# A rational convolution layer: third and fifth power in one VectorE instruction, and the sets of powers in steps inside the loop

## The chip, the core and the metric

The kernel runs on one core of a Trainium2 chip. The core has five engines that run side by side, each through its own instructions in order: TensorE (PE, matmuls, with PEld for its weight loads), VectorE (DVE), ScalarE (ACT), GpSimd (POOL) and SyncE (SP), which here only issues DMAs. They work on the on-chip memory SBUF (128 partitions)[...]. Larger buffers lie in DRAM and are reached by DMA.

The metric is the device time of one launch in microseconds (us). A profiled execution gives a trace: each instruction with its start, its duration and what ended the wait before it.

## What is computed

Four layers, each a residual step on an image batch of 8 x 16 x 128 x 128 in float32. The change is in the third, `L2` of the reference:

```python
x = x + _L2_conv_ref(_gn(x), L2_conv_A, L2_conv_Bc)

def _L2_conv_ref(x, A, Bc):          # K = 3, DEG_P = 6, DEG_Q = 4
    ...
    wins = jnp.stack([xp[:, :, i:i + H, j:j + W] for i in range(K) for j in range(K)])
    pw = wins[..., None] ** jnp.arange(DEG_P, dtype=x.dtype)
    P = jnp.einsum('pbchwi,fcpi->fpbchw', pw, A)
    Q = 1.0 + jnp.abs(jnp.einsum('pbchwi,fcpi->fpbchw', pw[..., 1:1 + DEG_Q], Bc))
    out = jnp.sum(P / Q, axis=(1, 3))
```

`_gn` normalizes the image in groups. For every pixel, window position, input channel and output channel there is a ratio of two polynomials of the normalized value; the ratios are summed over window positions and channels. The powers 1 to 5 of the normalized image are what the polynomials are made from.

## The kernel before

**Powers.** `x` stays in SBUF as 128 partitions (8 images by 16 channels) of 128 x 128 pixels. `powers(r0)` (line 929) makes a set: the powers 1 to 5 of two rows. Two small memsets on GpSimd blank the left and right edge; VectorE normalizes (L934); ScalarE squares for the second and the fourth power (L942, L944); GpSimd multiplies for the third and fifth (L943, L945). Five DMAs on SyncE's queue (L947) write the set into the DRAM tensor `yd2`, which has, for each group of four channels, the five powers of these as 20 rows. Each power has one SBUF tile, so two sets don't overlap. 64 sets make the image.

**Loads.** `turn(r0, g)` (line 955) reads ten rows of `yd2` back into four tiles `f`, with 16 DMAs on SyncE (L959), so that powers and channels lie on partitions. There are eight `f` tiles, two groups `g` of four; while one group is used, the other is loaded. Ten DMAs (L927) write a zero row above and below the image at the layer's start.

**The loop.** A turn is eight rows; it has two groups `g` (which images), two row blocks `k` of four rows, nine window positions `n`, two pairs of images `i`. Each combination is a `Couple`: 16 x 2 x 2 x 9 x 2 = 1152 of them. A couple is worked as follows, with quarter and half tiles of 128 x 2048 values:

- TensorE: `denominators` (L971, pd), `numerators` (L971, pn), and `over_channels` (L1062), which sums finished ratios into the accumulators.
- ScalarE: `absolute` twice (L1009, t from pd), `ln` and `exp` (L152, u), which make 1/Q as exp(-ln Q).
- VectorE: `step` (L1020, a product of t and u for a correction of that reciprocal), `times` twice (L1030), `ratio` (L1034).
- GpSimd: `correction` (L1043, v from t and u), made to wait for the next couple's step (`apart`, "shared port").

Tiles t and u have four buffers, v three; pd and pn one each. At the end of a row block VectorE adds the accumulator to `x` and takes statistics (L1074, L1075).

**What sets the order.** The program is not run in the order in which it is written: a scheduler orders each engine's instructions by their dependences. An order by hand is put on it with `in_turn(engine, ins)`, which ties an instruction to the one given before it under the same name. In the loop all of VectorE's four, ScalarE's four and TensorE's instructions of a couple are tied so ("dve", "act", "pe2"). The instructions of `powers` and `turn` are not tied to anything, and the trace has them where the scheduler put them. In the text five sets are made before the first load, three more before the loop, and then four at the first couple of each turn (line 1103), with `turn` at the first couple of each group.

Of the kernel before, what the change touches and what calls it, by code (L numbers as in the profile page):

```python
# [9 lines left out]
F32 = mybir.dt.float32  # L10
AF = mybir.ActivationFunctionType
# [5 lines left out]
B, C, H, W = 8, 16, 128, 128  # L17
BC = B * C
HW = H * W
HP, WP = H + 2, W + 2  # L20
# [80 lines left out]
def kernel(  # L101
# [20 lines left out]
    nc = tc.nc  # L122
# [6 lines left out]
    dram = ctx.enter_context(tc.tile_pool(name="scratch", bufs=1, space=DRAM))  # L129
# [11 lines left out]
    sets = {AF.Exp: "exp_ln", AF.Ln: "exp_ln", AF.Tanh: "sigmoid", AF.Sigmoid: "sigmoid"}  # L141
# [68 lines left out]
    def in_turn(engine, ins):  # L210

        if engine in chain:
            tc.add_manual_dep(ins, chain[engine].name, order, reason="in turn")
        chain[engine] = ins
        return ins
# [3 lines left out]
    for n in range(5):  # L219
        t = cpool.tile([BC, BC], F32, name=f"w1_{n}")  # L220
        nc.gpsimd.memset(t, 0.0)
        for b in range(B):
            r = slice(b * C, (b + 1) * C)
# [10 lines left out]
    with ExitStack() as l0:  # L234
        wp = l0.enter_context(tc.tile_pool(name="w0", bufs=1))
        with tc.tile_pool(name="x0", bufs=2) as xp:
# [6 lines left out]
            mean0, _, rs0, d0 = group_stats(bn0, "0")  # L243
# [25 lines left out]
        for a in range(2):  # L269
            src = aff_d[:, a : a + 1].rearrange("(d p g c) a -> p g c (d a)", p=2, g=2, c=C)  # L270
            for odd in range(2):
                for g in range(2):
                    for i in range(3):
                        r = 64 * (g ^ odd) + 16 * i
# [6 lines left out]
        for i in range(3):  # L281
            for g in range(2):
                r = slice(64 * g + i * 16, 64 * g + i * 16 + 16)
# [44 lines left out]
        act = l0.enter_context(tc.tile_pool(name="act0", bufs=1))  # L328
        tmp = l0.enter_context(tc.tile_pool(name="tmp0", bufs=1))
# [326 lines left out]
        for n in range(-2, NCH + 3):  # L656
# [62 lines left out]
            if any((new, old, ahead)):  # L719
                r = var.finish()  # L720
# [43 lines left out]
    with ExitStack() as l1:  # L764
# [50 lines left out]
        for s in range(4):  # L815
            for p in range(2):
                if 0 <= s - p < 3:
# [4 lines left out]
                    for g in range(2):  # L822
# [3 lines left out]
                            k_("image")[rows, 2 * s + g : 2 * s + g + 1],  # L826
                        )

        mean, dm, rs, _ = group_stats(bn1, "1")
        xmax = wp.tile([BC, 1], F32, name="xmax")  # L830
        nc.vector.tensor_reduce(xmax, top, AX.X, ALU.max)
# [82 lines left out]
    with ExitStack() as l2:  # L914
# [2 lines left out]
        gather = k_("gather").rearrange("p (k g m) -> p k g m", k=2, g=2)  # L917
        mean, _, rs, _ = group_stats(bn2, "2")


        yd2 = dram.tile([4 * B, 20, HP, WP], F32, name="yd2")
        yv = yd2.rearrange("g (i c) h w -> g i c h w", i=5)
        zt = wp.tile([BC, WP], F32, name="zt")
        nc.gpsimd.memset(zt, 0.0)
        for i in range(5):
            for r in (0, HP - 1):
                nc.sync.dma_start(yv[:, i, :, r, :], zt)  # L927

        def powers(r0):

            y = [tmp.tile([BC, 2, WP], F32, name=f"y{i}") for i in range(1, 6)]
            nc.gpsimd.memset(y[0][:, :, 0:1], 0.0)
            nc.gpsimd.memset(y[0][:, :, WP - 1 : WP], 0.0)
            nc.vector.tensor_scalar(  # L934
                y[0][:, :, 1 : 1 + W],
                x[:, r0 * W : (r0 + 2) * W].rearrange("p (a b) -> p a b", a=2),
                mean,
                rs,
                ALU.subtract,
                ALU.mult,  # L940
            )
            nc.scalar.activation(y[1], y[0], AF.Square)  # L942
            nc.gpsimd.tensor_mul(y[2], y[1], y[0])  # L943
            nc.scalar.activation(y[3], y[1], AF.Square)  # L944
            nc.gpsimd.tensor_mul(y[4], y[3], y[0])  # L945
            for i in range(5):
                nc.sync.dma_start(yv[:, i, :, 1 + r0 : 3 + r0, :], y[i])  # L947

# [1 line left out]
        for t in fs:  # L952
            nc.gpsimd.memset(t, 1.0)

        def turn(r0, g):
            for q in range(NP):
                for u in range(4):
                    lo = 32 * (u ^ (q % 2))
                    nc.sync.dma_start(  # L959
                        fs[g * NP + q][lo : lo + 20],  # L960
                        yd2[4 * (2 * q + g) + u, :, r0 : r0 + 10, :],
                    )
# [120 lines left out]
            for i in range(NP // 2)  # L1083
        ]
        count = len(couples)
        for r in range(0, 10, 2):
            powers(r)
        turn(0, 0)
        for r in range(10, 16, 2):
            powers(r)  # L1090
        for c in couples[:2]:
            for ab in range(2):
                c.denominators(ab)
# [4 lines left out]
        for m in range(count + 2):  # L1098
            before, c, then, far, next_ = (
                couples[i] if 0 <= i < count else None for i in range(m - 1, m + 4)  # L1100
            )
            if c:
                if (c.k, c.n, c.i) == (0, 0, 0):
                    if c.g == 0 and c.r0 + 16 < H:
                        for r in range(c.r0 + 16, c.r0 + 24, 2):
                            powers(r)
                    if c.r0 + 8 * c.g < H:
                        turn(c.r0 + 8 * c.g, 1 - c.g)
                c.exp()
                c.step()  # L1110
                c.numerators()
            if far:
                far.absolute(0)
                far.denominators(1)
            if then:
                then.ln()
            if m % 2:
                if m >= 3:
                    over_channels(couples[m - 3 : m - 1], 2)
            elif 2 <= m <= count:  # L1120
                over_channels(couples[m - 2 : m], 1)
                over_channels(couples[m - 2 : m], 0)
            if far:
                far.absolute(1)
            if next_:
                next_.denominators(0)
            if before:
                before.correction(c.stepped if c else before.stepped)
            if c:
                c.times()  # L1130
                c.ratio()
# [353 lines left out]
```

## Time and profile before

| | |
|---|---|
| Time, median of 3 runs | 10728.44 us (10727.74 to 10730.07) |
| The profiled execution | 10728.63 us |
| Its span in the trace | 10726.8 us |
| TensorE busy | 9016.0 us (84%) |
| VectorE busy | 8720.1 us (81%) |
| ScalarE busy | 8613.6 us (80%) |
| GpSimd busy | 5545.4 us (52%) |
| Granted TensorE clock, mean | 0.976 |

The page divides the span into 40 slices of 268 us and gives each engine's busy share in tenths (9 is 90% or more):

```profile
PE   4999999999998568888888888888888888888799
...
DVE  3555555555555569999999999999999999999977
ACT  2555555555554679999999999999999999999988
POOL 3655655555553555555555555555555555555522
```

Slices 0 to 12 are the first layer and the second; the rational layer begins in slice 13 and ends near slice 37; the rest is the fourth layer. The fourth section of the page names the chain that ended last, followed back from the last instruction:

```profile
DVE 42%; PE 24%; issue 21%; ACT 7%; POOL 3%; DMA 2%; SPq 1%; ACTq 0%; DVEq 0%; POOLq 0%
PE banks L360 18%; DVE u L1030 15%; DVE pn L1030 10%; DVE u L1034 8%; DVE y L518 2%; DVE t L1020 2%; PE pn L971 2%; PE pd L971 2%; PE acc L1334 1%; POOL y L527 1%; DVE x L538 1%; ACT u L152 1%; DMA yd<-y 1%; ACT hid L152 1%; SPq L1298 1%
```

Rows of the couple's instructions (line, engine, operation, output from inputs, shapes, count; busy time and mean of one in ns; idle time before them and what ended it):

```profile
L1043 POOL TENSOR_TENSOR v<-t,u 128x1280 f32<-128x1280 f32 x1152 | 3374.3, 2929 | 2990.1 <-DVE t L1020 2960.8
...
L1020 DVE SCALAR_TENSOR_TENSOR t<-t,u 128x2048 f32<-128x2048 f32 x1152 | 2637.5, 2289 | 34.8 <-ACT u L152 25.2
L1009 ACT ACTIVATE t<-pd 128x1024 f32<-128x1024 f32 x2304 | 2348.6, 1019 | 86.6 <-POOL v L1043 42.3
L152 ACT ACTIVATE u<-u 128x2048 f32<-128x2048 f32 x1152 | 2200.4, 1910 | 0.0
L152 ACT ACTIVATE u<-t 128x2048 f32<-128x2048 f32 x1152 | 2192.1, 1903 | 0.0
...
L1030 DVE TENSOR_TENSOR u<-pn,u 128x1280 f32<-128x1280 f32 x1152 | 1718.1, 1491 | 39.4
```

Busy times count an instruction from its start to its end; two in a row on one engine can overlap by some hundredths of a microsecond. The names in "out<-in" are those of the tiles; several layers have a tile y.

### The profile page before, as it was taken

The page shows a single profiled execution, that of the slowest core. Times are in us where ns is not written, and L with a number is a line of the kernel's source. Part 1 is how long each engine was busy: PE and PEld are TensorE (multiplying, and loading weights), DVE is VectorE, ACT ScalarE, POOL GpSimd, SP SyncE. Part 2 cuts the span into 40 slices and gives each one's busy share as a digit, 9 for nine tenths or more (in the row PEclk, how much of TensorE's full clock was granted, in tenths as well). Part 3 has the DMA queues.
Part 4 walks back from the last instruction along what each step waited for, and adds up shares of the span by engine and source line. Part 5 has one row for each costly group of instructions (what it writes and reads, how often), then busy time and mean ns, then how long its engine had stood idle before and what let it go on. Part 6 is the DMA issues. An engine that isn't in the chain of part 4 may idle for free.

```text
span 10726.8 us, 191623 instructions
## 1 busy us (share of the span) xinstructions
PE 9016.0 (84%) x81588; PEld 2440.6 (23%) x81588; DVE 8720.1 (81%) x6829; ACT 8613.6 (80%) x7107; POOL 5545.4 (52%) x2681
## 2 busy tenths in 40 slices
PE   4999999999998568888888888888888888888799
PEld 1222222222222112222222222222222222222222
DVE  3555555555555569999999999999999999999977
ACT  2555555555554679999999999999999999999988
POOL 3655655555553555555555555555555555555522
PEclk8999999999999789999999999999999999999999
DMA  1000000000001320000000000000000000000022
GB/s 50 14 14 12 16 13 14 15 13 13 16 10 44 96 87 8 14 7 8 14 8 7 14 8 8 14 7 8 14 8 8 14 8 7 14 8 8 7 62 61
DMA packets 189456, 205.04 MB, mean 19 GB/s; under 512 B 46776, under 2 KB 155448, under 8 KB 186552
## 3 DMA queue, kind: packets, MB, share of 16 engines
q1 hardware_dynamic: 179944, 190.68, 6.7%
q8 instruction: 641, 10.50, 0.4%
q10 hardware_dynamic: 8656, 2.11, 0.1%
q14 instruction: 215, 1.76, 0.1%
HBM read 107.15 MB, written 60.04 MB: 16 GB/s over the span
## 4 chain that ended last, share of the span: by engine, by line
DVE 42%; PE 24%; issue 21%; ACT 7%; POOL 3%; DMA 2%; SPq 1%; ACTq 0%; DVEq 0%; POOLq 0%
PE banks L360 18%; DVE u L1030 15%; DVE pn L1030 10%; DVE u L1034 8%; DVE y L518 2%; DVE t L1020 2%; PE pn L971 2%; PE pd L971 2%; PE acc L1334 1%; POOL y L527 1%; DVE x L538 1%; ACT u L152 1%; DMA yd<-y 1%; ACT hid L152 1%; SPq L1298 1%
## 5 line engine op out<-in xcount | busy, mean ns | idle before, releaser
L1043 POOL TENSOR_TENSOR v<-t,u 128x1280 f32<-128x1280 f32 x1152 | 3374.3, 2929 | 2990.1 <-DVE t L1020 2960.8
L971 PE MATMUL pd<-f,wb 32*64 32x512 f32 x18432 | 2518.4, 610 | 332.8 <-ACT t L1009 301.0
L1020 DVE SCALAR_TENSOR_TENSOR t<-t,u 128x2048 f32<-128x2048 f32 x1152 | 2637.5, 2289 | 34.8 <-ACT u L152 25.2
L1009 ACT ACTIVATE t<-pd 128x1024 f32<-128x1024 f32 x2304 | 2348.6, 1019 | 86.6 <-POOL v L1043 42.3
L152 ACT ACTIVATE u<-u 128x2048 f32<-128x2048 f32 x1152 | 2200.4, 1910 | 0.0
L152 ACT ACTIVATE u<-t 128x2048 f32<-128x2048 f32 x1152 | 2192.1, 1903 | 0.0
L971 PE MATMUL pn<-f,wa 32*64 32x512 f32 x18432 | 1324.8, 624 | 938.4 <-DVE u L1034 938.1
L1030 DVE TENSOR_TENSOR u<-pn,u 128x1280 f32<-128x1280 f32 x1152 | 1718.1, 1491 | 39.4
L152 ACT ACTIVATE hid<-banks 128x1024 f32<-128x1024 f32 x576 | 571.4, 1023 | 1046.6 <-PE banks L360 1044.7
L527 POOL TENSOR_TENSOR y<-y 128x1536 f32<-128x1536 f32 x256 | 894.7, 3495 | 830.9 <-DVE y L518 830.9
L1062 PE MATMUL acc<-u,const 128*32 128x512 f32 (+2 forms) x13824 | 1118.9, 456 | 0.0
L1030 DVE TENSOR_TENSOR pn<-pn,u 128x768 f32<-128x768 f32 x1152 | 1104.2, 959 | 0.0
L1034 DVE SCALAR_TENSOR_TENSOR u<-t,pn 128x768 f32<-128x768 f32 x1152 | 1087.6, 944 | 0.0
L518 DVE TENSOR_TENSOR y<-banks,vp 128x1536 f32<-128x1536 f32 x384 | 672.9, 1752 | 274.0 <-PE banks L360 271.8
L971 PEld LDWEIGHTS pd<-f,wb 32*64 32x64 f32 x18432 | 512.1, 131 | 1610.2 <-ACT t L1009 1548.7
L1062 PE MATMUL acc<-v,const 128*32 128x512 f32 (+1 forms) x9216 | 749.9, 443 | 1.5 <-POOL v L1043 1.5
L544 ACT ACTIVATE sq<-x 128x1024 f32<-128x1024 f32 x384 | 397.9, 1054 | 412.3 <-DVE x L538 289.7
L971 PEld LDWEIGHTS pn<-f,wa 32*64 32x64 f32 x18432 | 279.5, 131 | 1947.3 <-DVE u L1034 1936.7
L470 POOL TENSOR_TENSOR pd<-q,kp 128x1536 f32<-128x1536 f32 (+1 forms) x256 | 693.6, 2733 | 8.0 <-PE banks L360 7.2
L360 PE MATMUL banks<-att,const 32*128 32x512 f32 x2304 | 497.3, 667 | 173.5 <-DVE att L509 95.9
L360 PE MATMUL banks<-h,wfc 64*128 64x512 f32 (+1 forms) x3072 | 618.4, 631 | 14.5 <-DVE h L606 14.5
L606 DVE TENSOR_TENSOR h<-banks,x 128x1024 f32<-128x1024 f32 x192 | 232.6, 1211 | 435.5 <-ACT hid L152 230.4
(182 smaller groups left out, 8068.9 us busy)
## 6 DMA issues: line engine op xcount, KB each, us to landing
f<-yd SPq DMA_DIRECT2D x512, 101.6 KB
yd<-y SPq DMA_DIRECT2D x320, 130.0 KB
xin<-in_x SPq DMA_DIRECT2D x752, 32.0 KB
four<-sil SPq DMA_DIRECT2D x256, 65.0 KB
xj<-in_x SPq DMA_DIRECT2D x8, 1024.0 KB
xl<-in_x SPq DMA_DIRECT2D x32, 256.0 KB
x1d<-xl SPq DMA_DIRECT2D x32, 256.0 KB
x<-x1d SPq DMA_DIRECT2D x8, 1024.0 KB
```

Source lines behind the costliest of these rows:

```text
L152: ins = nc.scalar.activation(out_, in_, func, **kw).ins
L360: in_turn("pe", mm(*args, skip_group_check=True, **kw).ins)
L470: ins = nc.gpsimd.tensor_mul(t[:, :n].rearrange("p n (a b) -> p n a b", a=4), rows(self.q[d][:, k]).unsqueeze(1).to_broadcast([128, n, 4, W]),
L518: ins = nc.vector.tensor_mul(y.rearrange("p n (a b) -> p n a b", a=4), banks[:, 1:4].rearrange("p n (a b) -> p n a b", a=4), windows(v, j, 3),
L527: in_turn("pool", nc.gpsimd.tensor_add(self.y[k], self.y[k], y).ins)
L971: yield mm(p[64 * (u % 2) : 64 * (u % 2) + 64, u // 2], w[lo : lo + 32, q % 2, n].rearrange("p c f -> p (c f)"), fs[g * NP + q][lo : lo + ...
L1009: in_turn("act", nc.scalar.activation(self.t[:, ab], self.pd, AF.Abs).ins)
L1020: ins = nc.vector.scalar_tensor_tensor(self.t, self.t, 1.0, self.u, op0=ALU.add, op1=ALU.mult).ins
L1030: in_turn("dve", nc.vector.tensor_mul(u if cols.start else p, p, u).ins)
L1034: ins = nc.vector.scalar_tensor_tensor(u, t, 2.0, p, op0=ALU.subtract, op1=ALU.mult).ins
L1043: ins = nc.gpsimd.tensor_mul(self.v, t, u).ins
L1062: ins = mm(accs[k][32 * q : 32 * q + 32, lo % 512 : (hi - 1) % 512 + 1], gather[:, int(part == 1), g], flat(c.u)[:, ab, lo:hi] if src is N ...
```

## The change

- The five powers of a set lie in one tile instead of five. The third and fifth power are made by one VectorE instruction: powers 2 and 4 times power 1, repeated. GpSimd keeps the two edge memsets.
- `powers` becomes a generator of four steps: normalize; square; square; product and the five DMAs. Its VectorE and ScalarE instructions are tied with `in_turn` to the loop's.
- In the loop a set is begun in every half of a turn's group, that is for each `g` and `k`, with one step at each of the first four window positions, at the first pair of images, ahead of that couple's exponential and step.
- `turn` is called at the fifth window position of a group instead of the first.
- The first eight sets use buffers of the loop's tiles t and u, and go side by side, three, then two, then three. Two of their five DMAs each go to ScalarE's queue, and every second one of the first turn's loads.
- The zero rows are written before the second layer's statistics, and from a tile with five rows of zeros.

```diff
+        yd2 = dram.tile([4 * B, 20, HP, WP], F32, name="yd2")
+        yv = yd2.rearrange("g (i c) h w -> g c i h w", i=5)
+        zt = wp.tile([BC, 5, WP], F32, name="zt")
+        nc.gpsimd.memset(zt, 0.0)
+        for r in (0, HP - 1):
+            for i in range(5):
+                nc.sync.dma_start(yv[:, :, i, r, :], zt[:, i])
+
         mean, dm, rs, _ = group_stats(bn1, "1")
...
-        for i in range(5):
-            for r in (0, HP - 1):
-                nc.sync.dma_start(yv[:, i, :, r, :], zt)
...
-            y = [tmp.tile([BC, 2, WP], F32, name=f"y{i}") for i in range(1, 6)]
-            nc.gpsimd.memset(y[0][:, :, 0:1], 0.0)
-            nc.gpsimd.memset(y[0][:, :, WP - 1 : WP], 0.0)
-            nc.vector.tensor_scalar(
-                y[0][:, :, 1 : 1 + W],
+        def powers(r0, name):
+
+            if name:
+                y = tmp.tile([128, 2, 2, 512], F32, name=name, bufs=4)
+                y = y.rearrange("p a b c -> p (a b c)")[:, : 10 * WP]
+            else:
+                y = tmp.tile([128, 10 * WP], F32, name="y")
+            y = y.rearrange("p (i r w) -> p i r w", i=5, r=2)
+            nc.gpsimd.memset(y[:, 0, :, 0:1], 0.0)
+            nc.gpsimd.memset(y[:, 0, :, WP - 1 : WP], 0.0)
+            ins = nc.vector.tensor_scalar(
+                y[:, 0, :, 1 : 1 + W],
...
-            )
-            nc.scalar.activation(y[1], y[0], AF.Square)
-            nc.gpsimd.tensor_mul(y[2], y[1], y[0])
-            nc.scalar.activation(y[3], y[1], AF.Square)
-            nc.gpsimd.tensor_mul(y[4], y[3], y[0])
+            ).ins
+            yield in_turn("dve", ins)
+            yield in_turn("act", nc.scalar.activation(y[:, 1], y[:, 0], AF.Square).ins)
+            yield in_turn("act", nc.scalar.activation(y[:, 3], y[:, 1], AF.Square).ins)
+            ins = nc.vector.tensor_mul(
+                y[:, 2::2], y[:, 1::2], y[:, 0:1].to_broadcast([128, 2, 2, WP])
+            ).ins
+            in_turn("dve", ins)
             for i in range(5):
-                nc.sync.dma_start(yv[:, i, :, 1 + r0 : 3 + r0, :], y[i])
+                eng = nc.scalar if name and i % 2 else nc.sync
+                eng.dma_start(yv[:, :, i, 1 + r0 : 3 + r0, :], y[:, i])
+            yield
...
-        def turn(r0, g):
+        def turn(r0, g, engines=(nc.sync,)):
...
-                    nc.sync.dma_start(
+                    engines[u % len(engines)].dma_start(
...
-        for r in range(0, 10, 2):
-            powers(r)
-        turn(0, 0)
-        for r in range(10, 16, 2):
-            powers(r)
+
+        def together(sets):
+            for _ in range(4):
+                for c in sets:
+                    next(c)
+
+        together([powers(r, "tu"[r // 2 % 2]) for r in range(0, 6, 2)])
+        together([powers(r, "tu"[r // 2 % 2]) for r in range(6, 10, 2)])
+        turn(0, 0, (nc.sync, nc.scalar))
+        together([powers(r, "tu"[r // 2 % 2]) for r in range(10, 16, 2)])
...
-                if (c.k, c.n, c.i) == (0, 0, 0):
-                    if c.g == 0 and c.r0 + 16 < H:
-                        for r in range(c.r0 + 16, c.r0 + 24, 2):
-                            powers(r)
-                    if c.r0 + 8 * c.g < H:
-                        turn(c.r0 + 8 * c.g, 1 - c.g)
+
+                if (c.n, c.i) == (0, 0) and c.r0 + 16 < H:
+                    later = powers(c.r0 + 16 + 4 * c.g + 2 * c.k, None)
+                if c.i == 0 and c.n < 4 and c.r0 + 16 < H:
+                    next(later)
+                if (c.k, c.n, c.i) == (0, 4, 0) and c.r0 + 8 * c.g < H:
+                    turn(c.r0 + 8 * c.g, 1 - c.g)
                 c.exp()
                 c.step()
                 c.numerators()
```

More of the change, by code (lines that the diff above doesn't have):

```diff
@@ L918 @@
         mean, _, rs, _ = group_stats(bn2, "2")
[L921 to L924, printed above, removed]
-        for i in range(5):
-            for r in (0, HP - 1):
-                nc.sync.dma_start(yv[:, i, :, r, :], zt)
-        def powers(r0):
-            y = [tmp.tile([BC, 2, WP], F32, name=f"y{i}") for i in range(1, 6)]
-            nc.gpsimd.memset(y[0][:, :, 0:1], 0.0)
-            nc.gpsimd.memset(y[0][:, :, WP - 1 : WP], 0.0)
-            nc.vector.tensor_scalar(
-                y[0][:, :, 1 : 1 + W],
+        def powers(r0, name):
[9 more added lines that the diff above has]
+                y[:, 0, :, 1 : 1 + W],
                 x[:, r0 * W : (r0 + 2) * W].rearrange("p (a b) -> p a b", a=2),
```

## The prediction

> **What bounds the kernel now.** I read the slices of the page first: the rational layer fills the span from about 3540 to 10165 us, and inside it VectorE and ScalarE are at nine tenths, except in one early stretch. So I asked for busy time by window (columns: stretch, its length, busy time of TensorE, its weight loads, VectorE, ScalarE and GpSimd, granted clock, DMA share, GB/s):
>
> ```profile
> 3800.00:3900.00 100.00, 59.52 (x528) 14.63 (x520) 60.59 (x56) 65.69 (x70) 62.40 (x73) 0.83 0.30 101
> ...
> 6000.00:8000.00 2000.00, 1650.86 (x18689) 432.80 (x18681) 1979.98 (x1457) 1976.53 (x1438) 1051.19 (x359) 1.00 0.04 10
> ```
>
> Late in the layer VectorE and ScalarE are both 99% busy; early, nothing is over 66%. What differs early is the powers: the code issues four sets per turn, yet the rows of tile y (duration least/median/most, first and last start) show all 64 sets done by 3986 us:
>
> ```profile
> L934 DVE TENSOR_SCALAR y<-x,mean,rs x64: 409/414/1250, 3543.5 to 3977.3; 128x256 f32<-128x256 f32 x64
> ...
> L943 POOL TENSOR_TENSOR y<-y,y x64: 724/733/2539, 3546.4 to 3978.8; 128x260 f32<-128x260 f32 x64
> L945 POOL TENSOR_TENSOR y<-y,y x64: 721/734/2547, 3547.1 to 3985.2; 128x260 f32<-128x260 f32 x64
> ```
>
> The step of a couple (L1020) counts couples. Its row for three windows:
>
> ```profile
> L1020 DVE SCALAR_TENSOR_TENSOR t<-t,u x44: 2282/2291/2294, 3584.3 to 3986.6; 128x2048 f32<-128x2048 f32 x44
> ...
> L1020 DVE SCALAR_TENSOR_TENSOR t<-t,u x37: 2273/2292/2294, 3992.2 to 4195.8; 128x2048 f32<-128x2048 f32 x37
> ...
> L1020 DVE SCALAR_TENSOR_TENSOR t<-t,u x29: 2273/2291/2294, 10001.5 to 10157.2; 128x2048 f32<-128x2048 f32 x29
> ```
>
> The first 44 couples take 3992.2 - 3584.3 = 407.9 us, 9.27 each; the other 1107 intervals to 10157.2 take 6165.0, 5.57 each. The timeline of one early couple says why (start, duration, instruction, idle before it):
>
> ```profile
> 3804.08 2.29 DVE L1020 SCALAR_TENSOR_TENSOR t<-t,u 128x2048 f32<-128x2048 f32 x1
> 3804.43 2.54 POOL L945 TENSOR_TENSOR y<-y,y 128x260 f32<-128x260 f32 x1 [2.28 <-ACT y L944]
> ...
> 3807.13 3.05 POOL L1043 TENSOR_TENSOR v<-t,u 128x1280 f32<-128x1280 f32 x1
> ```
>
> A power product that starts under the step lasts 2.54 instead of 0.73 us and ends with it; GpSimd then reaches the correction (L1043) late, and ScalarE, which needs the correction's tile back, with it. Late couples show how tight that ring is:
>
> ```profile
> 6004.71 2.29 DVE L1020 SCALAR_TENSOR_TENSOR t<-t,u 128x2048 f32<-128x2048 f32 x1
> ...
> 6007.14 2.93 POOL L1043 TENSOR_TENSOR v<-t,u 128x1280 f32<-128x1280 f32 x1 [2.56 <-DVE t L1020]
> ...
> 6008.24 1.91 ACT L152 ACTIVATE u<-u 128x2048 f32<-128x2048 f32 x1
> ...
> 6010.10 1.02 ACT L1009 ACTIVATE t<-pd 128x1024 f32<-128x1024 f32 x1
> 6010.26 2.29 DVE L1020 SCALAR_TENSOR_TENSOR t<-t,u 128x2048 f32<-128x2048 f32 x1
> ```
>
> The exponential ends at 10.15 (us after 6000), the step that needs it starts at 10.26; the correction ends at 10.07, and the absolute value that reuses its buffer starts at 10.10. ScalarE's four instructions occupy about 5.5 us per couple, VectorE's four 5.5. Neither has room.
>
> **What the change removes.** (1) The 128 products on GpSimd, and with them the early stretch. With sets pinned into the loop, the first 44 intervals should cost 44 x 5.57 = 245.1, not 407.9: a gain of **163 us**. Bounds: 163 if the products are the whole cause; some 80 if the writes' DMA share of 0.30 there, or the sets' own VectorE and ScalarE work, is half of it. I take 163, since each early timeline couple has the late correction in it; the sets' own work is charged below.
>
> (2) The start. Before, five sets run one after another, 3.3 us apart, behind a single buffer; the first loads of f are issued at 3564.8 and the first matmul starts at 3568.0. Side by side, the products are done by some 3553 (ten squares of 0.42 and five products of 0.70 instead of five rounds). But 10 of the 25 writes and half of the 16 loads move to ScalarE's queue, where the eight loads of L809 took 8.38 us to issue; eight alike (L808) took 5.14 on SyncE. So ten writes and eight loads keep ScalarE some 18 us, its squares for the next sets and its first absolute values queued behind them. The edge memsets still wait for the 9.2 us of f memsets. Bounds: 8 us gained, 4 lost. I take **3 us gained**.
>
> **What it adds.** 56 sets now stand in the loop's own order, one per 18 couples. Per set:
> - VectorE, the normalization: 0.41 us, before the step. A busy VectorE starts its next instruction 0.08 before the last one's end (the step lasts 2.29, its successor starts 2.21 after it), so 0.34. It was on VectorE before, but early, in idle time.
> - VectorE, the product of 520 elements. No row is this shape. L1030 takes 959 ns for 768 and 1491 for 1280 elements: 1.04 ns each and 160 fixed, so 0.70, net 0.63. Bounds: 0.54 at 1.04 ns with nothing fixed, 0.85 if the strided broadcast costs a fifth more.
> - ScalarE, two squares of 0.42, each ahead of an exponential; net 0.32 (an absolute value lasts 1.02 and its successor starts 0.92 later). What queues behind: the exponential, and behind it the step. With 0.02 or so to spare, 0.30 each, 0.60. Bounds: nothing, if ScalarE had run ahead; 0.84 in full.
> - GpSimd keeps two memsets of 0.10, in gaps of 2.56 us. SyncE's five writes (0.54 each) go past no other work: it has only the 16 loads per half turn. These loads move eight couples later, with 28 couples x 5.57 = 156 us left until their tiles are read; the cover is gone only if they took over 150 us.
> - The zero rows move under layer 1: ten issues, 6.4 us, behind weights that SyncE has issued by 3486.7. Nothing, unless SyncE takes them before the weight loads that hold layer 1's first correction; then up to 6 us lost.
>
> 0.34 + 0.63 + 0.60 = 1.57 us. One nearer row prices an insertion as a whole. L1074 and L1075 (0.68 + 0.69) stand in front of a step twice per turn, and the timeline around 6167 shows what follows:
>
> ```profile
> 6173.80 1.02 ACT L1009 ACTIVATE t<-pd 128x1024 f32<-128x1024 f32 x1 [1.24 <-POOL v L1043]
> ...
> 6174.03 1.32 PE L971 MATMUL pn<-f,wa 32*64 32x512 f32 x16 [1.93 <-DVE u L1034]
> ...
> 6175.06 2.00 PE L971 MATMUL pd<-f,wb 32*64 32x512 f32 x8
> ```
>
> The steps are 6.79 apart there, 1.29 over the usual 5.5. But TensorE had idled 1.93 us instead of 0.8, its next eight matmuls took 2.00 us instead of 1.06, ScalarE waited 0.48 for them and the step two couples on was 0.58 late. Over the starts of all steps, 17 of 31 such places show this second loss, 0.45 us on average. **The clock** is therefore the rule to weigh. The Trainium skill (TensorE: Matmul & The Clock Gate, What's actually happening) has the clock halved after an idle window of about 3.4 us: by it, idle gaps of 0.8 + 0.3 to 0.6 us cost nothing, and a set stays at 1.57. The row has slow matmuls after 1.93 us. Scaled by the four shorter gaps it might be up to 1 us per set; I take 0.13, near the rule, as these gaps stay well under 1.9: **1.70 us per set**, 56 x 1.70 = **95 us**.
>
> A second rule speaks for one half of the change and against the other. The skill (SBUF — State Buffer, SBUF: two separate sides) gives VectorE and GpSimd one port pair, locked for a whole instruction when VectorE reads two SBUF tensors. Row 3804.43 agrees. The new product is such an instruction; if the correction held the pair, it would wait up to 2.93 us, 56 x 2.93 = 164 us. But it stands where the step stands, and there the correction ends at 10.07 and the step starts at 10.26. I charge nothing.
>
> **Sum**, against the profiled execution's 10728.63 us (span 10726.8; the median of three runs is 10728.44, so the two can be used alike): 10728.6 - 163 - 3 + 95 = **10658 us**.
>
> **Rivals.**
> A, the forecast: 10658, 10635 to 10680 by its costs.
> B, the squares fall into ScalarE's waits and only VectorE pays: 0.97 per set, 54 us: 10617. For it: VectorE's own idle before L1020 is only 34.8 us in 1152 couples. Against it: ScalarE is as full as VectorE.
> C, insertions echo as L1074's do, 2.5 us per set, 140 us: 10703.
> D, slower: the clock falls at each of four insertions per set, with 0.8 us lost each, or the new product meets the correction. 1.57 + 3.2 = 4.8 per set, 267 us: 10830. It decides from 166 / 56 = 3.0 us per set. For it: the 2.00 us row. Against it: shorter gaps.
> E, the change does not do what it says: only VectorE and ScalarE work is pinned, memsets and writes are not, and if the early stretch owes half to DMA, 80 us come back: 10729 - 83 + 95 = 10741, no visible change.
>
> **How the numbers follow.** Chances: A 0.60, B 0.13, C 0.13, D 0.08, E 0.06. The range takes A, B and most of C: 10612 to 10705. Less than 0.2% (21 us) can't be told from no change. Faster: A, B, most of C, 0.84; the same: E with some of C, 0.06; slower: D and a little of E, 0.10.
>
> **What would show it.** Right: step starts 5.5 to 5.6 apart from the first couple; per 18 couples four intervals longer by 0.3, 0.3, 0.3 and 0.6; no GpSimd products of y; a product near 0.70 us. Wrong: products of 2 us or more; many 2.00 us matmul groups after insertions (D); slow early couples although the products are gone (E); ScalarE idle over 10 us at the start.

## The result, and the profile after

| | before | after |
|---|---|---|
| Median of 17 runs each, us | 10728.44 | 10709.14 (10700.72 to 10717.02) |
| Ratio to before, 95% interval | | 0.9982 (0.9974 to 0.9989) |
| Profiled execution, us | 10728.63 | 10710.04 |
| Its span, us | 10726.8 | 10708.2 |

The kernel is 19 us faster, where 70 were forecast, and lies 4 us above the forecast's range. VectorE's slices on the page of the changed kernel, in tenths of 268 us each, show that the early stretch is gone:

```profile
DVE  3555555555555899999999999999999999999977
```

Slices 13 and 14 (counted from 0), 5 and 6 tenths before, are 8 and 9. The windows of busy time (columns as in the prediction) say it more sharply:

```profile
3600.00:3850.00 250.00, 204.60 (x2268) 52.83 (x2272) 244.15 (x180) 241.69 (x182) 128.46 (x50) 0.99 0.06 16
...
6000.00:8000.00 2000.00, 1630.15 (x18240) 421.25 (x18240) 1965.85 (x1461) 1939.78 (x1442) 1030.45 (x389) 0.99 0.06 16
```

Early, VectorE is busy for 98% of the time (244.15 of 250 us); before, it was 61% in the early window that the prediction shows. Late, ScalarE has *lost* ground: 1939.78 of 2000 us instead of 1976.53, although it now does the squares there as well. An engine that was full, got more work and is less busy waits for something new. The page's rows of the couple (columns as before) say what:

```profile
L1053 POOL TENSOR_TENSOR v<-t,u 128x1280 f32<-128x1280 f32 x1152 | 3373.0, 2928 | 2986.5 <-DVE t L1030 2868.6
...
L1030 DVE SCALAR_TENSOR_TENSOR t<-t,u 128x2048 f32<-128x2048 f32 x1152 | 2688.6, 2334 | 97.4 <-ACT u L152 91.0
L1019 ACT ACTIVATE t<-pd 128x1024 f32<-128x1024 f32 x2304 | 2352.7, 1021 | 206.1 <-POOL v L1053 145.7
```

The absolute value (L1009 before, now L1019) waits 145.7 us for the correction instead of 42.3. The step (now L1030) has a mean of 2334 ns instead of 2289, though nothing in it changed. A mean can hide a few long ones, and the step's own row, with least, median and most, shows that it does:

```profile
L1030 DVE SCALAR_TENSOR_TENSOR t<-t,u x1152: 2274/2291/4593, 3591.0 to 10138.4; 128x2048 f32<-128x2048 f32 x192
```

Most steps are as before, and some last up to 4.59 us. Their places come from the starts of the 1152 steps. A half of a turn's group has 18 couples, and each set's parts stand ahead of the same couples of it. Means of the interval from the step at a place to the next one, in us, over steps 72 to 999; the last column is an experiment told below:

| place, and what of a set stands there | before | after | edges blanked once |
|---|---|---|---|
| 17: normalization | 5.55 | 5.79 | 5.79 |
| 1: first square | 6.18 | 6.34 | 6.33 |
| 3: second square | 5.72 | 5.87 | 5.87 |
| 5: product | 5.55 | 6.08 | 6.07 |
| 7: nothing in the text | 5.55 | **6.86** | 5.58 |
| 8: nothing | 5.49 | 5.71 | 5.47 |
| all 18 | 100.23 | 102.72 | 101.19 |

The four edited places grow by 0.15 to 0.53. The largest growth, 1.31, is at a place where the text puts nothing. The timeline of one such place (start, duration, instruction, idle before it and what ended it):

```profile
4035.60 0.69 DVE L950 TENSOR_TENSOR y<-y 128x520 f32<-128x520 f32 x1
...
4036.21 2.29 DVE L1030 SCALAR_TENSOR_TENSOR t<-t,u 128x2048 f32<-128x2048 f32 x1
4036.32 1.17 SPq L956 DMA_DIRECT2D yd<-y  x2
...
4039.28 0.10 POOL L937 MEMSET y<- 128x2 f32 x1 [3.79 <-DMA yd<-y]
...
4039.42 2.91 POOL L1053 TENSOR_TENSOR v<-t,u 128x1280 f32<-128x1280 f32 x1
...
4041.67 2.81 DVE L1030 SCALAR_TENSOR_TENSOR t<-t,u 128x2048 f32<-128x2048 f32 x1
...
4042.36 1.02 ACT L1019 ACTIVATE t<-pd 128x1024 f32<-128x1024 f32 x1 [1.30 <-POOL v L1053]
```

Read it from the memset. It belongs to the *next* set, whose normalization comes only twelve couples later. It isn't tied to anything, and the scheduler put it in GpSimd's order right after the last set's product (L950) and writes. There is one tile y, and the memset may overwrite it only when the five writes of the last set have read it: it waits 3.79 us. GpSimd works in order, and the correction stands behind the memset. The step ended at 4036.21 + 2.29 = 4038.50; the correction, usually right behind, starts at 4039.42. It still runs when the next step comes at 4041.67, and that step then lasts 2.81 us. ScalarE waits 1.30 us for the correction's tile. The view of waits from 4200 to 9000 us (who, for whom, sum, times, the longest) shows it as a habit:

```profile
POOL y L937 <- DMA yd<-y: 151.3, 35, 5.6
ACT t L1019 <- POOL v L1053: 120.7, 129, 3.1
...
POOL y L937 <- DVE pn L1040: 47.2, 12, 4.0
```

These are 35 waits, 4.3 us each on average, by an instruction of 0.10 us. Twelve more, 3.9 us each, the view puts down to VectorE's product; each of them, too, ends about 2 us after the last of a set's writes was issued. Of such a wait GpSimd would have stood idle for its usual 2.5 us anyway; what goes beyond that delays the correction, by 0.9 us in the timeline (4039.42 against 4038.50).

Where the time went, by the starts of the steps, all from profiled executions:

| us | before | after | change | forecast |
|---|---|---|---|---|
| span's start to the first step | 3584.3 | 3591.0 | +6.7 | -3 |
| first 44 intervals | 407.9 | 251.6 | -156.3 | -163, and some sets' cost |
| other 1107 intervals | 6165.0 | 6295.9 | +130.9 | +95, less those sets |
| last step to the span's end | 569.6 | 569.8 | +0.2 | 0 |

### The profile page after: what moved, and what is told of

It is laid out like the page before. It is cut to its first block, busy times and chain, and to the rows that moved or that the text cites. A ratio compares the mean times of both kernels' runs of the same rounds, so it can differ in the third digit from the quotient of the medians.

```text
span 10708.2 us, 191588 instructions
## 1 busy us (share of the span) xinstructions
PE 9027.5 (84%) x81588; PEld 2426.8 (23%) x81588; DVE 8799.1 (82%) x6893; ACT 8603.2 (80%) x7107; POOL 5415.3 (51%) x2553
## 4 chain that ended last, share of the span: by engine, by line
DVE 36%; PE 24%; issue 17%; ACT 13%; POOL 5%; DMA 2%; SPq 2%; ACTq 0%; DVEq 0%; POOLq 0%
PE banks L360 18%; DVE u L1040 11%; DVE pn L1040 8%; DVE u L1044 6%; ACT u L152 5%; POOL v L1053 4%; DVE t L1030 3%; ACT t L1019 3%; DVE y L518 2%; PE pd L981 2%; PE pn L981 2%; DMA yd<-y 1%; POOL y L527 1%; DVE x L538 1%; PE acc L1350 1%
## 5 line engine op out<-in xcount | busy, mean ns | idle before, releaser
L1030 DVE SCALAR_TENSOR_TENSOR t<-t,u 128x2048 f32<-128x2048 f32 x1152 | 2688.6, 2334 | 97.4 <-ACT u L152 91.0
L1019 ACT ACTIVATE t<-pd 128x1024 f32<-128x1024 f32 x2304 | 2352.7, 1021 | 206.1 <-POOL v L1053 145.7
```

The lines of the kernel that those rows point to most:

```text
L1019: in_turn("act", nc.scalar.activation(self.t[:, ab], self.pd, AF.Abs).ins)
L1030: ins = nc.vector.scalar_tensor_tensor(self.t, self.t, 1.0, self.u, op0=ALU.add, op1=ALU.mult).ins
```

## The experiments

Each edit is told against the kernel named. Ratios are to the kernel before, on the same chip.

### The memsets tied in their place

The changed kernel, with GpSimd given an order by hand too:

```diff
-            nc.gpsimd.memset(y[:, 0, :, 0:1], 0.0)
-            nc.gpsimd.memset(y[:, 0, :, WP - 1 : WP], 0.0)
+            for w in (0, WP - 1):
+                in_turn("pool", nc.gpsimd.memset(y[:, 0, :, w : w + 1], 0.0).ins)
...
-                ins = nc.gpsimd.tensor_mul(self.v, t, u).ins
+                ins = in_turn("pool", nc.gpsimd.tensor_mul(self.v, t, u).ins)
```

> The changed kernel with its two edge memsets per set tied into GpSimd's order, where the text has them: just before a set's normalization, 12 couples after the writes they wait for. Theory (the memsets, put right behind the last set's product, hold GpSimd until that set's writes have landed, 180.1 us in 42 waits, and the correction with it): the two intervals at that place are 1.31 and 0.2 us too long, 55 times; without them about 10709 - 82 = 10627 us, and all couples but the four insertions at 5.5. Rival (those intervals are the echo of the new product, a slow TensorE clock after it, and the memset only happens to stand there): no change, 10700 to 10715.

Measured: 10622.1 us, 0.9910 (0.9895 to 0.9924). The same instructions in another order on one engine, and 87 us are gone between the medians, 82 between the profiled spans (10708.2 and 10626.0). The medians of different experiments come partly from different chips, on which the kernel before took from 10723.31 to 10730.72 us; so differences of a few microseconds between them are read from the traces.

### The edges blanked once

The changed kernel, with a lasting tile for y. Its edges are never overwritten by the sets, so two memsets before the loop are enough:

```diff
+        ring = wp.tile([128, 10 * WP], F32, name="y")
+        blank(ring.rearrange("p (i r w) -> p i r w", i=5, r=2))
...
-                y = tmp.tile([128, 10 * WP], F32, name="y")
+                y = ring
...
-            nc.gpsimd.memset(y[:, 0, :, 0:1], 0.0)
-            nc.gpsimd.memset(y[:, 0, :, WP - 1 : WP], 0.0)
+            if name:
+                blank(y)
```

> The changed kernel with one lasting tile y for the sets in the loop, whose edges are blanked once, so that no memset is left in the loop. Theory (memsets waiting for the writes): as the tied memsets, about 10627 us, at most 2 us apart from them. Rival (echo of the product): 10700 to 10715. If the tile y's single buffer itself were the wait (normalization against the last set's writes), it would show as VectorE waiting before L939's successor, and this kernel would keep the loss too.

Measured: 10622.45 us, 0.9909 (0.9895 to 0.9924). Two ways of getting rid of the wait agree within 0.4 us, so it is the wait that costs, and not the memsets' own 0.20 us a set. The page's rows of this kernel for step and correction:

```profile
L1061 POOL TENSOR_TENSOR v<-t,u 128x1280 f32<-128x1280 f32 x1152 | 3375.3, 2930 | 3138.6 <-DVE t L1038 3138.6
...
L1038 DVE SCALAR_TENSOR_TENSOR t<-t,u 128x2048 f32<-128x2048 f32 x1152 | 2635.0, 2287 | 69.7 <-ACT u L152 58.5
```

The step is back at 2287 ns, and all of the correction's 3138.6 us of idle time ends with the step, as it should. The same window of waits as above has ScalarE's wait at half:

```profile
ACT t L1027 <- POOL v L1061: 63.0, 127, 1.0
```

The other 1107 intervals take 6216.5 us here: 79.4 of the changed kernel's 6295.9 are the memsets' wait, and 4.6 more lie in the first 44 (251.6 against 247.0). What the others take over the kernel before, 51.5 us, is the price of the sets: 0.96 each by the table of places (101.19 - 100.23).

### The products on GpSimd again

The kernel with the edges blanked once, and in it the very operations that the prediction blamed for the early stretch:

```diff
-            ins = nc.vector.tensor_mul(
-                y[:, 2::2], y[:, 1::2], y[:, 0:1].to_broadcast([128, 2, 2, WP])
-            ).ins
-            in_turn("dve", ins)
+            nc.gpsimd.tensor_mul(y[:, 2], y[:, 1], y[:, 0])
+            nc.gpsimd.tensor_mul(y[:, 4], y[:, 3], y[:, 0])
```

> The steps in the loop alone: as the kernel with the edges blanked once, but the third and fifth power are two products on GpSimd again, as before the change. If it was the rush of sets at the start that cost, and not where the products run: the products lie in GpSimd's gaps of 2.5 us or hold one step for 0.7 us each, 10600 to 10675. If GpSimd products are what cost, wherever they are (163 us over 56 sets is 2.9 us per set): 2.9 x 56 = 163 us above a kernel with no cost, 10710 to 10740. My theory: each product stands before a correction, starts under a step or just ahead of one, and costs 1 to 2.5 us: 10660 to 10740, slower than on VectorE.

Measured: 10598.6 us, 0.9886 (0.9869 to 0.9902). The theory that these products must cost falls; the rival held, and by a little more than its own numbers. GpSimd's two products are 24 us *cheaper* than VectorE's one. The rows of tile y of this kernel (least, median and most duration, first and last start) show that they are undisturbed:

```profile
L958 POOL TENSOR_TENSOR y<-y x55: 724/737/758, 3705.0 to 9142.6; 128x260 f32<-128x260 f32 x55
L959 POOL TENSOR_TENSOR y<-y x55: 722/737/749, 3716.7 to 9154.8; 128x260 f32<-128x260 f32 x55
```

None lasts over 0.76 us, where before the change the most was 2.55. Each follows a square that is tied to its place, so it comes when GpSimd is in its gap of 2.5 us, just before a step that the square delays anyway; 48 steps still last longer than usual, by 3.0 us in all. Place 5 of the table goes from 6.07 to 5.57.

### The VectorE product alone

The kernel before, with one tile for the five powers and the third and fifth power on VectorE, but all untied and at the old calls:

```diff
-            y = [tmp.tile([BC, 2, WP], F32, name=f"y{i}") for i in range(1, 6)]
+            y5 = tmp.tile([BC, 5, 2, WP], F32, name="y")
+            y = [y5[:, i] for i in range(5)]
...
-            nc.gpsimd.tensor_mul(y[2], y[1], y[0])
...
-            nc.gpsimd.tensor_mul(y[4], y[3], y[0])
+            nc.vector.tensor_mul(
+                y5[:, 2::2], y5[:, 1::2], y5[:, 0:1].to_broadcast([BC, 2, 2, WP])
+            )
```

> The one VectorE product alone: the kernel before, with the third and fifth power in one VectorE instruction, and one tile for a set; sets stay untied, so that the scheduler still puts all of them at the start. If products under the step were the cause of the 9.27 us couples: about 10728 - 163 + 60 = 10625 us, early couples at 6 to 7 us. If the memsets' wait for the last set's writes is a cause of its own (my theory): early couples stay at 7.5 to 9 us and the time at 10670 to 10720.

Measured: 10718.84 us, 0.9994 (0.9985 to 1.0002). The first 44 intervals take 347.0 us instead of 407.9, but only 41 sets are made in them instead of 56; the rush lasts longer, and the others take 6211.9 instead of 6165.0. So moving the products alone to VectorE leaves the early couples slow, and gains next to nothing. The memsets were in question next: here too they wait for the writes, 87.4 us in 41 waits between 3600 and 3990 us.

### Before, with the edges blanked once

The kernel before, whose tile of the first power lasts:

```diff
+        ring = wp.tile([BC, 2, WP], F32, name="y1")
+        nc.gpsimd.memset(ring[:, :, 0:1], 0.0)
+        nc.gpsimd.memset(ring[:, :, WP - 1 : WP], 0.0)
...
-            y = [tmp.tile([BC, 2, WP], F32, name=f"y{i}") for i in range(1, 6)]
-            nc.gpsimd.memset(y[0][:, :, 0:1], 0.0)
-            nc.gpsimd.memset(y[0][:, :, WP - 1 : WP], 0.0)
+            y = [ring] + [tmp.tile([BC, 2, WP], F32, name=f"y{i}") for i in range(2, 6)]
```

> The kernel before, with power 1 in one lasting tile whose edges are blanked once: no memset of GpSimd waits for a set's writes any more, the products stay on GpSimd and the sets stay untied at the start. If the products under the step make the 9.27 us couples by themselves: still 8.5 us or more over the first 44, 10700 to 10728. If the memsets' wait is what makes them (as the VectorE product alone, which kept memsets and gained 4 us, suggests): 7 us or less over the first 44 to 60 couples, 10630 to 10670.

Measured: 10731.43 us, 1.0000 (0.9992 to 1.0009), the first 44 intervals 415.6 us. The memsets are not the cause either, by themselves.

### VectorE product and edges once, both untied

The kernel of the VectorE product alone, with its tile made lasting in the same manner.

> The VectorE product alone (sets untied, all at the start; 10718.8 us), now with one lasting tile whose edges are blanked once, so that neither product nor memset of a set is left on GpSimd. If the memsets' wait for a set's writes (87.4 us in 41 waits over the early stretch) is what kept that kernel slow: the early couples fall from 8.2 to 6.5 or 7 us, time 10640 to 10680. If the rush itself costs, because VectorE and ScalarE instructions of untied sets stand in their in-order queues where the loop has no room and wait there for each other (VectorE waited 32.3 us for squares): early couples stay at 7.5 us or more, 10700 to 10725. I hold the second likelier by now, since blanking once did nothing for the kernel before.

Measured: 10733.96 us, 1.0005 (0.9996 to 1.0013), above both forecasts, the first 44 intervals 416.3. With neither products nor memsets left on GpSimd in the rush, the early couples are as slow as ever. The timeline of an early couple shows a part of what holds them:

```profile
3703.68 3.21 POOL L1047 TENSOR_TENSOR v<-t,u 128x1280 f32<-128x1280 f32 x1 [7.50 <-DVE t L1024]
3704.19 2.86 DVE L937 TENSOR_SCALAR y<-x,mean,rs 128x256 f32<-128x256 f32 x1
...
3714.92 2.26 DVE L947 TENSOR_TENSOR y<-y 128x520 f32<-128x520 f32 x1 [1.35 <-ACT y L946]
```

A normalization of usually 0.41 us starts just after a step, while the correction runs, and lasts 2.86 until the correction's end; a product of usually 0.69 lasts 2.26. Whichever engine has them, operations of the sets that fall beside the correction are held by it, or hold it.

How this reaches the couples is seen on ScalarE. The kernel before, 4 us ahead of the row that the prediction read:

```profile
3800.34 0.41 DVE L934 TENSOR_SCALAR y<-x,mean,rs 128x256 f32<-128x256 f32 x1 [3.76 <-POOL y L945]
...
3800.92 0.42 ACT L942 ACTIVATE y<-y 128x260 f32<-128x260 f32 x1 [5.20 <-DVE y L934]
```

The normalization waits for the last set's product, the square for the normalization, and behind the square stand the couples' absolute values and exponentials, since each engine works in order. The waits from 3590 to 3990 us, first before the change, then in this experiment:

```profile
DVE y L934 <- POOL y L945: 135.1, 53, 4.2
...
ACT y L942 <- DVE y L934: 117.2, 51, 5.2
```

```profile
ACT y L945 <- DVE y L937: 74.1, 35, 3.8
...
ACT y L945 <- issue: 51.4, 18, 4.2
...
DVE y L947 <- DMA yd<-y: 0.3, 1, 0.3
```

Over the first 44 intervals ScalarE waits 120.8 us before the sets' first squares in the kernel before and 125.6 us here; its squares themselves take 47.0 in both. These sums, 168 and 173 us, are about what the stretch takes over the 247.0 us of the kernel with the edges blanked once: 161 and 169. The same sum fits the two untied kernels between: 174 against 169 with the edges blanked once, 96 against 100 for the VectorE product alone. The changed kernel has no wait before a square there. So the early stretch reads as ScalarE's wait in its own order, whichever engine makes a set late; the writes' DMA traffic, the prediction's other suspect, holds this kernel for 0.3 us. This is an account from the traces: no run moves the squares alone.

### The product made twice

The kernel with the edges blanked once; every set in the loop makes its product a second time, with the same result:

```diff
-            ins = nc.vector.tensor_mul(
...
+            for _ in range(1 if name else 2):
+                ins = nc.vector.tensor_mul(
...
```

> The kernel with edges once and the VectorE product (10622.5 us), in which each set in the loop makes that product twice, the second time over the same values. If a product costs what VectorE takes for it (0.69 us, 0.63 net of overlap; the interval there is 0.50 to 0.53 longer): 10622 + 56 x 0.6 = 10656, 10650 to 10660. If it also slows TensorE's clock, as the 1.37 us insertion at the end of a row block does in half of the cases: 56 x (0.6 + 0.2 to 0.45), 10665 to 10680.

Measured: 10693.48 us, 0.9964 (0.9951 to 0.9977), 71 us above the kernel that makes it once between the medians and 66 between the profiled spans, or 1.2 per set: more than any theory gave. The first product costs 0.52, the second 0.74 at its own place (6.81 against 6.07) and 0.45 two couples on (6.03 against 5.58). The second part is TensorE's. Two such places in the timeline of this kernel, one and then the other:

```profile
5783.41 1.12 PE L990 MATMUL pn<-f,wa 32*64 32x512 f32 x16 [1.95 <-DVE u L1053]
...
5784.32 1.06 PE L990 MATMUL pd<-f,wb 32*64 32x512 f32 x8
...
5884.85 1.25 PE L990 MATMUL pn<-f,wa 32*64 32x512 f32 x16 [1.96 <-DVE u L1053]
...
5885.81 2.00 PE L990 MATMUL pd<-f,wb 32*64 32x512 f32 x8
```

After the same idle time, eight matmuls take 1.06 us once and 2.00 the other time. The windows of just these two groups (columns as in the prediction) have the granted clock at 1.00 and at 0.50:

```profile
5784.32:5785.38 1.06, 1.06 (x20) 0.25 (x16) 1.06 (x1) 1.06 (x1) 0.00 (x0) 1.00 0.00 0
5885.81:5887.81 2.00, 2.00 (x20) 0.39 (x16) 2.00 (x2) 1.64 (x1) 0.67 (x1) 0.50 0.03 8
```

So a second insertion at one place is not priced like the first.

### All powers on GpSimd

The kernel with the products on GpSimd; in the loop the squares are GpSimd products too, one at each window position, tied in GpSimd's order with the corrections:

```diff
-            yield in_turn("act", nc.scalar.activation(y[:, 1], y[:, 0], AF.Square).ins)
-            yield in_turn("act", nc.scalar.activation(y[:, 3], y[:, 1], AF.Square).ins)
-            nc.gpsimd.tensor_mul(y[:, 2], y[:, 1], y[:, 0])
-            nc.gpsimd.tensor_mul(y[:, 4], y[:, 3], y[:, 0])
+            for o, a, b in ((1, 0, 0), (2, 1, 0), (3, 1, 1), (4, 3, 0)):
...
+                    ins = nc.gpsimd.tensor_mul(y[:, o], y[:, a], y[:, b]).ins
+                    if not name:
+                        in_turn("pool", ins)
```

> As the kernel with products on GpSimd (10598.6 us), but the two squares are GpSimd products too, so that a set is one VectorE instruction and four GpSimd ones, one per window position, each tied behind the correction before it. Theory (a GpSimd product that starts when the correction ends, some 0.1 us before the next step, holds that step for what is left of it, and was free so far only because the square on ScalarE delayed the same step anyway): each of the four costs 0.4 to 0.6 us, less the 0.3 us saved at two squares: 10598 + 56 x (4 x 0.5 - 0.6) = 10676, 10640 to 10700. Rival (products in GpSimd's gaps are free, squares on ScalarE cost 0.3 each): 10598 - 56 x 0.45 = 10573, 10565 to 10585.

Measured: 10640.77 us, 0.9916 (0.9899 to 0.9932): 42 us slower than with ScalarE's squares between the medians, 37 between the profiled spans, at the lower edge of what the theory gave. The timeline of one place:

```profile
5741.12 2.92 POOL L1064 TENSOR_TENSOR v<-t,u 128x1280 f32<-128x1280 f32 x1 [2.54 <-DVE t L1041]
...
5744.01 0.73 POOL L960 TENSOR_TENSOR y<-y 128x260 f32<-128x260 f32 x1
...
5744.26 2.63 DVE L1041 SCALAR_TENSOR_TENSOR t<-t,u 128x2048 f32<-128x2048 f32 x1
```

The product runs until 4.74 (us after 5740), the step comes at 4.26 and lasts 0.34 longer than its 2.29. GpSimd is idle for half of the time, but without a square to delay the step, its gap ends when the step starts. 180 steps are lengthened so, by 52 us in all.

### The start's DMAs on SyncE

The kernel with the products on GpSimd, with the first eight sets' writes and the first turn's loads all on SyncE's queue, as before the change:

```diff
-                eng = nc.scalar if name and i % 2 else nc.sync
+                eng = nc.sync
...
-        turn(0, 0, (nc.sync, nc.scalar))
+        turn(0, 0)
```

> The kernel with steps in the loop, edges once and products on GpSimd (10598.6 us), with all writes and loads of the start on SyncE's queue again. Theory (ScalarE is held at the start by issuing: its first absolute value waited until the last of its ten-odd issues was out, 17 us, although the matmuls before it were done at 3571): the first step comes at 3584 to 3587 us instead of 3592.4, the time 5 to 8 us lower, 10591 to 10594. Rival (the first absolute value waits for the writes out of the buffer it reuses, whoever issues them): first step no earlier, time the same or some us higher.

Measured: 10600.19 us, 0.9877 (0.9863 to 0.9892): no gain that can be told. From the first normalization to the first step it takes 41.8 us instead of 46.2, but the first normalization came 2.6 us later in that profile, and the first step is only 1.8 us earlier.

### The zero rows at their old place, alone and with the start's DMAs

The kernel with the products on GpSimd, with the ten zero-row DMAs written where they were before the change (and the small tile for them); then the same with the edit just shown.

> The kernel with steps in the loop, edges once and products on GpSimd (10598.6 us), with the zero rows written at the rational layer's start again, as before the change. In the kernels with the moved zero rows the second layer takes some 2.5 us longer from its first statistics to its gates (16.8 us against 14.1). If the moved writes and their memset are the cause: the first normalization 2 to 4 us earlier after the first layer's end, the time 10594 to 10597. If they lie beside other work: no difference, 10597 to 10601.

> As the last, and all writes and loads of the start on SyncE's queue too. The start took 41.8 us from the first normalization to the first step that way, 45.8 in the changed kernel, 40.8 before the change. Expected: both gains add up, 10590 to 10595. Rival (the second layer's end moves by as much from run to run, and hides it): 10596 to 10601.

Measured: 10599.93 us, 0.9884 (0.9866 to 0.9902), with four runs between 10587 and 10622; and 10591.72, 0.9874 (0.9858 to 0.9889). The zero rows show no effect. Both together are 7 us below the products on GpSimd, with overlapping intervals, so the time alone does not settle it. The traces do better. The changed kernel's start:

```profile
3568.14 3.17 PE L981 MATMUL pd<-f,wb 32*64 32x512 f32 x8 [24.35 <-DMA f<-yd]
...
3576.36 2.05 ACTq L956 DMA_DIRECT2D yd<-u  x2
...
3578.46 1.02 ACT L1019 ACTIVATE t<-pd 128x1024 f32<-128x1024 f32 x1 [17.23 <-DMA yd<-t]
```

And that of the last kernel:

```profile
3564.93 7.87 SPq L974 DMA_DIRECT2D f<-yd  x16
...
3568.09 3.63 PE L986 MATMUL pd<-f,wb 32*64 32x512 f32 x8 [27.20 <-DMA f<-yd]
...
3571.81 1.02 ACT L1024 ACTIVATE t<-pd 128x1024 f32<-128x1024 f32 x1 [20.74 <-PE pd L986]
```

The first matmul comes at the same time. The first absolute value comes 6.65 us later where ScalarE issues DMAs, because it stands behind writes that ScalarE issues until 3576.36 + 2.05 = 3578.41. (The row puts the wait down to a write out of tile t; but where SyncE issues the same writes the absolute value starts right behind its matmuls, at 3571.81 after 3571.72.) The first step is at 3591.0 and at 3584.4. Against the kernel with the zero rows alone (3591.4), 4.8 of the 7.0 us lie between the first normalization and the first step (42.1 instead of 46.9), and 2.2 before it, where the two don't differ: the layers ahead scatter by such amounts. This last kernel, at 10591.72, is the fastest of all that ran, 1.3% below the kernel before.

## Why the prediction was wrong

The direction was right and the size was not. Point by point:

- **The step that failed** is "GpSimd keeps two memsets of 0.10, in gaps of 2.56 us", costed at nothing. The prediction named the cover but did not ask what each memset waits for: it overwrites a tile that five DMAs still read. The duration of 0.10 us says nothing of a wait of 4 us, longer than the gap, in an in-order queue with the correction behind it. The runs put it at 84 us by the starts of the steps (79.4 in the later couples and 4.6 in the first 44), some 1.5 per set (102.72 - 101.19), and at 87 us between the medians (10709.1 against 10622). The working had weighed a product that meets the correction (164 us, charged at nothing), yet not a memset that delays it.
- **The early stretch**: 163 us were forecast to go, 156.3 went, with the cost of two or three sets still inside. The size was right by luck, for the reason was wrong. The products on GpSimd were blamed, through late corrections and ScalarE's wait for the correction's tile. In the trace of the kernel before ScalarE has no such wait in that stretch; it waits 120.8 us before the sets' first squares. The product of row 3804.43 did not end with the step either, but 0.60 us after it (3806.97 against 3806.37). With the products on GpSimd behind squares that are tied the kernel is fastest, and without them, untied, the stretch stays (416.3 us). What took it away is the order by hand. It both spreads the sets, one per 18 couples instead of more than one per couple, and puts each part ahead of a step; which of the two does it was not tried.
- **The sets**: 0.96 us each, not 1.70. The normalization added 0.24 (forecast 0.34), the product 0.52 (0.63), the squares 0.16 and 0.15 (0.30 each); the 0.13 for the clock did not appear: from 4100 to 10000 us the trace has 15 stretches at half clock before the change and 3 in the kernel with the edges blanked once. A square costs 0.32 where no end of a row block falls into its couple's neighbourhood. In the other half of the cases the couple behind L1074 and L1075 takes 6.8 us with or without the first square, and the echo two couples on is gone, in the second square's place. Rival B's 0.97 per set was right in its sum but not by its mechanism, since VectorE's part is smaller and ScalarE does pay.
- **The start**: 3 us gained were forecast, 6.7 lost. The fear was right that ScalarE's first absolute values would stand behind its DMAs, the balance was not.
- **No meeting of product and correction, no halved clock at every insertion** (rival D): right. The product lasts 0.69 (forecast 0.70). By the starts of the steps the second loss behind L1074 comes at 16 of the 31 places, not 17, with 0.44 us on average over all 31.

Put the measured terms into the sum, and it closes: 10658 + 84 for the memsets + 10 for the start - 41 for the sets (56 x 0.74) = 10711, against a profiled execution of 10710.04. Without the memsets' wait the kernel takes 10622, which lies inside the range of the prediction, 36 below its middle because the sets cost less than charged.

## What to carry to other kernels

When a step is moved, ask of every instruction that it issues what it must wait for and who stands behind it on its engine: the reuse of a single buffer is such a wait, and an instruction of 0.1 us can hold an engine for 4, longer than the gap of 2.5 that it was to fit into. If only part of a sequence is tied into an order by hand, the scheduler may place the rest a dozen couples early, so tie it too or take it out of the loop. A busy engine that got more work and is less busy, and a growth at a place where nothing was inserted, are the two symptoms to look for.

## What the runs showed of the hardware

**TensorE after a pause.** Counted over 4100 to 10000 us by the idle time before the numerators: after about 2.0 us (in the trace's modelled ends), the next eight matmuls were slow, 2.0 us instead of 1.06, in 15 of 27 cases in the kernel before and in 27 of 54 with the product made twice. At up to some 1.6 us none was slow in these two, of about 2000, though only 27 of those were near 1.6. At the memsets' place of the changed kernel, with 1.2 us there and other pauses next to it, 20 of 53 were. The traces put this down to the clock: in the same stretch they record 15 and 27 periods at a granted clock of 0.50, each 3.4 us long, and every slow group falls on one of them. The Trainium skill (TensorE: Matmul & The Clock Gate, What's actually happening) gives an idle window of about 3.4 us before the clock halves; here pauses of 1.93 to 1.96 us were followed by half clock in 42 of 81 cases. What tells one such pause from the other the runs do not show.

**VectorE and GpSimd beside each other.** In two of the timelines above the one that came second was held for no longer than what was left of the first: the step for 0.34 us by a product that ended 0.48 us after it began (2.63 instead of 2.29), a normalization for 2.45 us by a correction that ended 2.70 us after it began (2.86 instead of 0.41). There the overlap sets what such a meeting costs.
